# Band scores of a two-axis transformer block: every 128-key block in two 64-key halves

## The chip, the cores and the metric

One core of a Trainium2 chip runs the whole kernel. The metric is the device time of one launch in microseconds (us). Five engines run their own instruction streams side by side and meet at semaphores: TensorE (PE, matrix products; its weight loads are listed apart as PEld), VectorE (DVE), ScalarE (ACT), GpSimd (POOL) and the queue that issues transfers (SP).

## The reference, cut to what matters

The input `x` is 2 x 256 x 128 x 128 in fp32 (batch, time, band, channel). Three residual steps follow one another, each with its own layer norm: attention along time with a causal mask, attention along the 128 bands with a band mask, and a feed-forward with 512 hidden channels and gelu.

```python
bm = _band_mask(x.shape[2], BAND)      # 0 where |i - j| <= 16, else -inf
xt = _ln(x, ln_t_w, ln_t_b).transpose(0, 2, 1, 3)
x = x + _mha(xt, t_wi, t_bi, t_wo, t_bo, H_T, cm).transpose(0, 2, 1, 3)
xf = _ln(x, ln_f_w, ln_f_b)
x = x + _mha(xf, f_wi, f_bi, f_wo, f_bo, H_F, bm)
xn = _ln(x, ln_n_w, ln_n_b)
h = jax.nn.gelu(xn @ w1.T + b1, approximate=False)
x = x + (h @ w2.T + b2)
```

There are 4 heads of 32 channels. In the attention over bands, each of the 2 x 256 time steps is a sequence of 128 bands. A query attends only to keys within 16 bands of it, so a set of 64 keys meets at most 64 + 16 queries inside its block of 128.

## The kernel before, in words

Everything is fp32. The work is cut into groups of four sequences, 512 tokens each (`NT = 4` blocks of `P = 128`). First come 128 groups of attention over time (`OverTime`), then, for each run of 32 time steps, 8 groups of attention over bands (`OverBands`) followed by 8 groups of feed-forward (`FeedForward`); there are 16 such runs, so 128 groups of each kind. The band and feed-forward runs begin near 941 us of the profiled execution.

`BoundedPath.run` (L1057) writes the order out by hand as a software pipeline. Each step `n` of its loop does the scores of group `n`, the weighting of group `n-1`, the output product of group `n-2`, the projections of group `n+1`, and on VectorE the normalisation of a group three or more steps ahead. `InOrder` (L871) pins every instruction to that program order on its engine, so each engine works off its list as written.

For a band group the steps matter in this order:

- `queries_keys`, `take_query`, `take_key`, `values`, `take_values` (L576 to L602): TensorE projects the queries, keys and values; ScalarE copies them from PSUM to `qT`, `kT` and `v`. `qT` and `kT` hold head `h` in partitions 32h to 32h+31 and the 512 tokens along the free axis.
- `scores` (L764): TensorE multiplies keys by queries, one PSUM bank per head. A product for head `h` reads 32 rows. Its keys are the stationary operand and its queries the moving one, and the keys decide which PSUM partitions are written.
- `first_function` (L778): for the last head, VectorE clamps the scores and adds the mask in PSUM (a SCALAR_TENSOR_TENSOR, bank<-bank,band). ScalarE then exponentiates the four heads one after the other into `pf`.
- `first_mask` (L788): for the other three heads GpSimd sets the entries outside the band to zero by two affine selects each.
- `weigh` (L802) in the next step: TensorE sums the weights (`pf,ones`) and multiplies them into the values (`pf,v`).
- `invert` and `divide` (L607, L620): ScalarE takes ln and exp for the reciprocal (`r`), and VectorE does three passes that end in `oT`.
- `output` and `finish` (L635, L641) in the step after: TensorE multiplies `oT` by the output weights, and VectorE adds the result to the residual.

Between these, VectorE normalises a later group (four TENSOR_SCALAR into `xh`), transposes 32 x 32 squares into `z` (STREAM_TRANSPOSE), and in some steps takes the statistics of a group five steps ahead (`stats`, then `mv`). SP writes `z` to DRAM (`turned`) and reads it back as `xnT`.

A run's bands are numbered 0 to 7 here. In the loop the statistics of the feed-forward group `n+5` are taken in the steps of bands 3 to 7, because those feed-forward groups begin right after band 7. For the first run the band statistics, too, fall into its own steps (`due`, L1074).

PSUM has eight banks, handed out in turn by `bank` (L918). A band step takes ten turns: four for the scores, two held for a later output and query, and one each for `rp`, `op`, `kp` and `vp`. Thus a bank comes back one step later, and a product into it waits until its last reader is done. At the end of a run, where a feed-forward takes four turns and the projections are absent, `rp` of band 7 lands on the bank of `rp` of band 6.

In the scores before, the first and the last of the four blocks are done in two halves of 64 keys, each against 80 queries. The two middle blocks are done whole, 128 keys against 128 queries:

```python
for i, part in ((0, HALF), (1, P), (2, P), (3, HALF)):
    reach = 0 if part == P else BAND
```

Of the kernel before, what the change touches and what calls it, by code (L numbers as in the profile page):

```python
# [19 lines left out]
P = 128  # L20
H = 4
D = 32
BAND = 16
EPS = 1e-5
NEG = -1e38
NT = 4
# [6 lines left out]
HALF = P // 2  # L33
# [613 lines left out]
def rows_of(h):  # L647
    return slice(h * D, (h + 1) * D)
# [109 lines left out]
class OverBands(Attention):  # L758
# [5 lines left out]
    def scores(self, heads):  # L764
        path = self.path
        self.sp = {h: path.bank([P, NT * P], "sp") for h in heads}
        for i, part in ((0, HALF), (1, P), (2, P), (3, HALF)):
            reach = 0 if part == P else BAND
            for e in range(0, P, part):
                a = i * P + (e - reach if e else 0)  # L770
                q, keys = slice(a, a + part + reach), slice(i * P + e, i * P + e + part)
                for h in heads:
                    r = rows_of(h)
                    path.tensor.matmul(
                        self.sp[h][e : e + part, q], self.kT[r, keys], self.qT[r, q], start=True, stop=True
                    )

    def first_function(self):  # L778
# [459 lines left out]
```

## Time and profile before

| | us |
|---|---|
| median of 3 runs | 2713.04 (2712.95 to 2713.34) |
| profiled execution, its own time | 2711.64 |
| its span, first to last instruction | 2709.8 |
| PE busy | 2682.0 (99%) |
| DVE busy | 2195.4 (81%) |
| POOL busy | 1952.3 (72%) |
| ACT busy | 1854.5 (68%) |

The page comes from one execution of the program. A group of instructions is named by engine, operation, output and inputs, with partitions x elements; `32*64` on a matmul means 32 contracted rows and 64 stationary columns. Almost all instructions carry the line L881, the line of the helper that pins the order, so they are told apart by names and shapes. An fp32 product appears as two records of a weight load and two of a matmul. A matmul's end is modelled, so the starts of the records are the firm times. The granted TensorE clock was 0.998.

### The profile page before, as it was taken

To read this page: it belongs to the slowest core of one execution; us is meant where nothing else is said; L and a number is where in the kernel's file an instruction comes from. 1 tells how busy PE (TensorE), PEld (TensorE's weight loads), DVE (VectorE), ACT (ScalarE), POOL (GpSimd) and SP (SyncE) were. 2 spreads that over 40 slices of the span, in tenths; PEclk is the share of its full clock that TensorE was granted. 3 is DMA by queue.
4 is the path that set the end of the run, shared out by engine and by line. 5 is a ranking of instruction groups with operands and counts; after the bars stand their busy time and mean duration, and the time that the engine had idled before them with its cause. 6 is when DMAs were issued, how large, how long until landed. Compare 5 with 4: busy or idle time off the path is not lost.

```text
span 2709.8 us, 152534 instructions
## 1 busy us (share of the span) xinstructions
PE 2682.0 (99%) x66614; PEld 1805.8 (67%) x66614; DVE 2195.4 (81%) x6708; ACT 1854.5 (68%) x3620; POOL 1952.3 (72%) x2297
## 2 busy tenths in 40 slices
PE   7999999999999999999999999999999999999998
PEld 5666666666666666666666666666666666666666
DVE  6888989888988896977968769778687696886874
ACT  5999999999999865564655745646556466465563
POOL 4999999999999885766666657566676575665762
PEclk9999999999999999999999999999999999999999
DMA  5556555555555444444445444454454444544533
GB/s 147 149 150 157 148 151 153 155 148 149 152 154 150 124 112 122 124 111 122 115 119 128 112 120 120 112 131 108 119 131 108 124 121 111 131 108 117 132 94 82
DMA packets 471495, 346.83 MB, mean 128 GB/s; under 512 B 43296, under 2 KB 405152, under 8 KB 470816
## 3 DMA queue, kind: packets, MB, share of 16 engines
q1 hardware_dynamic: 469568, 335.92, 48.0%
q8 instruction: 524, 8.59, 1.4%
q14 instruction: 155, 1.27, 0.2%
q10 hardware_dynamic: 1248, 1.05, 0.2%
HBM read 169.03 MB, written 167.77 MB: 124 GB/s over the span
## 4 chain that ended last, share of the span: by engine, by line
PE 87%; DVE 10%; DMA 1%; ACT 1%; issue 0%; POOL 0%; SPq 0%; DVEq 0%; ACTq 0%
PE bank L881 87%; DVE xh L881 2%; DVE bank L881 2%; DVE stats L881 1%; DVE u L881 1%; DVE z L881 1%; DVE x L881 1%; DVE oT L881 1%; DMA xnT<-turned 1%; DVE mv L881 0%; DMA x<-in_x 0%; ACT p L881 0%; DVE vy L881 0%; DMA rows_sb<-in_rows 0%; DVE res L881 0%
## 5 line engine op out<-in xcount | busy, mean ns | idle before, releaser
L881 ACT ACTIVATE hT<-bank,b 128x512 f32<-128x512 f32 x512 | 347.1, 688 | 526.5 <-PE bank L881 507.7
L881 POOL TENSOR_SCALAR_AFFINE_SELECT pf<-pf 128x512 f32<-128x512 f32 x768 | 478.6, 638 | 289.5 <-ACT pf L881 263.0
L881 DVE TENSOR_SCALAR xh<-x,mv,rstd 128x160 f32<-128x160 f32 x1536 | 597.0, 431 | 14.3
L881 PEld LDWEIGHTS bank<-w2T_sb,hT 128*32 128x32 f32 x16384 | 457.1, 110 | 63.2 <-issue 39.7
L881 PE MATMUL bank<-xnT,wf 128*32 128x512 f32 x4096 | 488.7, 594 | 3.0 <-ACT p L881 3.0
L881 PE MATMUL bank<-w2T_sb,hT 128*32 128x128 f32 x16384 | 474.3, 273 | 0.2 <-ACT hT L881 0.2
L881 PE MATMUL bank<-xnT,w1f 128*32 128x512 f32 x4096 | 472.7, 592 | 0.0
L881 ACT ACTIVATE p<-bank 128x512 f32<-128x512 f32 (+1 forms) x1024 | 430.7, 494 | 38.4 <-PE bank L881 27.2
L881 POOL TENSOR_SCALAR_AFFINE_SELECT p<-p 128x1024 f32<-128x1024 f32 (+2 forms) x384 | 365.2, 951 | 86.0 <-ACT p L881 77.6
L881 DVE TENSOR_TENSOR res<-bank,res 128x512 f32<-128x512 f32 x256 | 175.9, 687 | 288.5 <-PE bank L881 229.8
L881 PE MATMUL bank<-qT,kT 32*64 32x80 f32 (+5 forms) x14336 | 363.5, 288 | 3.8 <-DVE oT L881 2.4
L881 PEld LDWEIGHTS bank<-qT,kT 32*64 32x64 f32 (+1 forms) x14336 | 288.8, 138 | 85.5 <-ACT kT L881 49.0
L881 PEld LDWEIGHTS bank<-wf,xnT 128*32 128x32 f32 x8192 | 233.6, 110 | 157.4 <-issue 102.8
L881 POOL TENSOR_TENSOR p<-p,p 128x512 f32<-128x512 f32 x256 | 324.5, 1289 | 10.7
L881 ACT ACTIVATE pf<-bank 128x512 f32<-128x512 f32 x512 | 264.5, 602 | 92.7 <-PE bank L881 92.1
L881 DVE BATCH_NORM_STATS2 stats<-x 128x6 f32<-128x128 f32 x1536 | 326.5, 275 | 0.4 <-DMA x<-in_x 0.4
L881 DVE STREAM_TRANSPOSE z<-xh 128x512 f32<-128x512 f32 x384 | 273.3, 712 | 13.5
L881 PEld LDWEIGHTS bank<-xnT,w1f 128*32 128x32 f32 x4096 | 150.5, 110 | 193.9 <-issue 168.7
L881 POOL TENSOR_TENSOR rstd<-rstd,mhalf 128x4 f32<-128x4 f32 x248 | 257.0, 1036 | 20.7
L881 PE MATMUL bank<-wf,xnT 128*32 128x128 f32 x8192 | 271.6, 273 | 0.0
L881 PE MATMUL bank<-wn,oT 128*32 128x128 f32 x8192 | 271.5, 273 | 0.0
L881 POOL TENSOR_SCALAR rstd<-mv 128x4 f32<-128x4 f32 x248 | 56.8, 229 | 297.1 <-DVE mv L881 296.6
(97 smaller groups left out, 3654.4 us busy)
## 6 DMA issues: line engine op xcount, KB each, us to landing
turned<-z SPq DMA_DIRECT2D x1536, 64.0 KB, 2.4
xnT<-turned SPq DMA_DIRECT2D x384, 256.0 KB, 3.0
x<-in_x SPq DMA_DIRECT2D x128, 256.0 KB, 4.2
x<-res SPq DMA_DIRECT2D x256, 128.0 KB, 2.5
x<-x SPq DMA_DIRECT2D x128, 256.0 KB, 4.3
out<-res SPq DMA_DIRECT2D x256, 128.0 KB, 2.5
w1T_sb<-in_w1T ACTq DMA_DIRECT2D x1, 256.0 KB, 6.0
w2T_sb<-in_w2T ACTq DMA_DIRECT2D x1, 256.0 KB, 7.1
```

Source lines behind the costliest of these rows:

```text
L881: return self.tc.keep_in_program_order(emit(*args, **kwargs))
```

## The change

Only `OverBands.scores` changes. All four blocks are now done in two 64-key halves against 80 queries: the first half meets queries 0 to 79 of its block, the second queries 48 to 127. Per group that makes 32 products of 32*64 in place of 16 of 32*64 and 8 of 32*128. The loop stays block by block, then half by half, then the four heads. The order of all other instructions is the same on every engine, and the products of the attention over time keep their own table.

```diff
-        for i, part in ((0, HALF), (1, P), (2, P), (3, HALF)):
-            reach = 0 if part == P else BAND
-            for e in range(0, P, part):
-                a = i * P + (e - reach if e else 0)
-                q, keys = slice(a, a + part + reach), slice(i * P + e, i * P + e + part)
+        for i in range(NT):
+            for e in range(2):
+                keys = slice(e * HALF, (e + 1) * HALF)
+                a = i * P + e * (HALF - BAND)
+                q = slice(a, a + HALF + BAND)
                 for h in heads:
                     r = rows_of(h)
                     path.tensor.matmul(
-                        self.sp[h][e : e + part, q], self.kT[r, keys], self.qT[r, q], start=True, stop=True
+                        self.sp[h][keys, q], self.kT[r, i * P + e * HALF : i * P + (e + 1) * HALF], self.qT[r, q],
+                        start=True, stop=True,
                     )
```

In the middle blocks, the corners of a bank that no product writes any more keep what the bank held before; the clamp with the mask and the two selects cover them, as they did in the first and last block.

## The prediction

> **What bounds the kernel now.** I read the page first, for which engine is full.
>
> ```profile
> PE 2682.0 (99%) x66614; PEld 1805.8 (67%) x66614; DVE 2195.4 (81%) x6708; ACT 1854.5 (68%) x3620; POOL 1952.3 (72%) x2297
> PE 87%; DVE 10%; DMA 1%; ACT 1%; issue 0%; POOL 0%; SPq 0%; DVEq 0%; ACTq 0%
> ```
>
> TensorE is full over the span and carries most of the chain that ended last, but VectorE carries a tenth of it. So the question is where. In a band step of a run's middle (the starts of the tensor records from 1527.098 to 1533.736 us) TensorE never pauses: scores 1305 ns, `pf,ones` 883, `pf,v` 873, output 873, queries and keys 1717, values 987; 6.638 us a step. The same step in the list of VectorE's instructions in order of time:
>
> ```profile
> 1528.73 0.70 DVE L881 SCALAR_TENSOR_TENSOR bank<-bank,band 128x512 f32<-128x512 f32 x1
> 1529.34 1.60 DVE L881 TENSOR_SCALAR xh<-x,mv,rstd 128x160 f32<-128x160 f32 x4
> 1530.97 0.71 DVE L881 STREAM_TRANSPOSE z<-xh 128x512 f32<-128x512 f32 x1
> 1531.61 0.83 DVE L881 BATCH_NORM_STATS2 stats<-x 128x6 f32<-128x128 f32 x4
> 1532.35 0.36 DVE L881 BATCH_NORM_AGGREGATE mv<-stats 128x2 f32<-128x6 f32 x4
> 1532.63 0.66 DVE L881 TENSOR_TENSOR x<-bank,x 128x512 f32<-128x512 f32 x1
> 1533.21 0.69 DVE L881 TENSOR_TENSOR bank<-bank,r 128x512 f32<-128x512 f32 x1
> 1533.93 0.69 DVE L881 SCALAR_TENSOR_TENSOR u<-bank,r 128x512 f32<-128x512 f32 x1
> 1534.66 0.69 DVE L881 TENSOR_TENSOR oT<-bank,u 128x512 f32<-128x512 f32 x1
> 1535.39 0.70 DVE L881 SCALAR_TENSOR_TENSOR bank<-bank,band 128x512 f32<-128x512 f32 x1
> ...
> 1554.60 0.69 DVE L881 TENSOR_TENSOR oT<-bank,u 128x512 f32<-128x512 f32 x1
> 1555.21 1.60 DVE L881 TENSOR_SCALAR xh<-x,mv,rstd 128x160 f32<-128x160 f32 x4
> ```
>
> No line names an idle time: VectorE is as full as TensorE. From `oT` to the next instruction it takes 0.73 us at 1534.66 but only 0.61 at 1554.60, where nothing is waited for. So about 0.1 us of the step is a wait for the scores, and VectorE's own step is 6.66 - 0.12 = 6.54. A second reading agrees: in the thirteenth run the mask starts 677, 579, 469 and 377 ns after the scores' end in four successive steps, so VectorE, once late, gains 0.10 a step. This holds for bands 3 to 7, which carry the statistics; earlier steps lack 1.02 us of them and do show idle time.
>
> Last, the chain between 1520 and 1570 us, at the end of the run:
>
> ```profile
> 1522.05 0.04 issue
> 1522.09 0.70 DVE bank L881
> ...
> 1553.87 0.70 DVE u L881
> 1554.58 0.14 issue
> 1554.71 15.34 PE bank L881 x389
> ```
>
> From the mask of band 3 to `u` of band 6 the chain stays on VectorE. Then `pf,ones` of band 7, which needs the bank that `u` read, waits for it: 740 ns from the last record before it, where this kind of product is otherwise followed at 382. All 16 runs have this gap (711 to 816).
>
> **What the Trainium skill says.** TensorEngine Tiling (Array Packing), Key Properties: a change of tiling mode drains TensorE, while tiles of one mode work independently. The trace agrees. The last record before the scores starts 203 ns before their first, against 92 at a boundary without a change; the middle blocks start 158 after the last record of the first block. TensorE: Matmul & The Clock Gate, LDWEIGHTS, has a load take its columns over 1.2 GHz: 53 ns for 64, 107 for 128. The second batch of records of the first block starts 120 ns after the first batch, which is 53 + 67 (two passes of 80 columns at the page's 2.4 GHz); in the middle blocks 213 = 107 + 107, and then 112, the load being hidden. The same page, under "Wait — 56ns, not 53.3ns?", has a floor of about 25 ns from matmul to matmul. Here the eight tiles' records start 6.7 ns apart in a batch, so a batch contradicts it; a rival below asks whether a long series does.
>
> **The change, part by part.**
>
> Removed: 16 records of 32*128 and two mode changes inside the scores. By starts, the 1305 ns are 324 (first block and the way out of it), 657 (middle blocks and out) and 324 (last block and out to `pf,ones`).
>
> Added: 32 records of 32*64 with 80 columns. All 64 records now run in one mode: eight batches of eight tiles. The first batch to the second is 120 as now. The last batch to `pf,ones` is 204 as now (1509.107 to 1509.311). Between lie six batch intervals that the trace does not have. I take 72: two passes of 80 are 66.7, plus the 5 that separate 112 from 106.7. The time scores support hidden loads, since their closing 64-column products follow one another on a tile at 58 ns where two passes are 53. The lower bound is 67. The upper is 120, nothing hidden. Sum: 120 + 6 x 72 + 204 = 756, so **0.549 us less per band group**; with 120, 0.261; with 67, 0.579.
>
> Moved: nothing. ScalarE, VectorE, GpSimd and SP keep their instructions and their order, and no transfer is added. No wait is added; the existing ones meet a TensorE that comes earlier. The exponentials start 0.2 us after the scores end; the copy of `v` before them ends 0.75 after the scores start, just before the new end at 0.756. So they follow. `kT`, for which the scores wait, depends on products whose length stays. GpSimd needs 5.2 us a step (3.94 of selects, 1.27 for `rstd`), below any step considered. The saved 0.549 would be complete at the end if VectorE kept up.
>
> It does not. TensorE's step becomes 6.09, VectorE's stays 6.54 in bands 3 to 7. Steps 0 to 2 need at most 5.52 of VectorE, so it follows TensorE up to the mask of band 3: four scores, 4 x 0.549 = 2.20. From there it runs alone and gains only what it waits now, four times 0.10 (masks of bands 4, 5, 6, 7). `u` of band 6 thus comes 2.60 earlier, and so does `pf,ones` of band 7. TensorE's remaining 4 x 0.549 - 0.4 = 1.8 turns into waits: first for a score bank read by `finish`, or for `oT`, which now precedes its product by 1.4; then at `pf,ones`. Nothing later in the run changes: `oT` of band 7 still precedes its product by 0.8, and feed-forward steps leave VectorE spare time.
>
> If VectorE's cover were gone, the price of those waits would be 0, and the run would gain 8 x 0.549 = 4.39.
>
> First run: its own statistics make VectorE late already. Its masks start up to 1.48 us after the scores and TensorE stalls in two score sections (2470 and 2052 ns). The mask of band 1 is the last that waits for TensorE, so I count 2 x 0.549 = 1.1. Sum: 15 x 2.60 + 1.1 = 40.1. Since VectorE's own delays now show (0.35 in the thirteenth run), I take off 0.5: **39.6 us**. Against the profiled execution's 2711.64 that is 2672.0. The median lies 1.4 above that execution: **2673.5**.
>
> **Rivals.**
>
> - *Loads are not hidden, or products come slower in a long series* (intervals up to 120): 4 x 0.261 + 0.4 = 1.44 a run; 15 x 1.44 + 0.5 = 22, time 2691. For it: no series of 80-column batches on 64-column tiles exceeds two now. Against: the 58 ns above.
> - *VectorE is not the limit*, and the run gains 4.39: 16 x 4.39 = 70, time 2643. The gap at `pf,ones` in all 16 runs and the 0.10 recovered speak against it.
> - *Nothing arrives*: 32 products take what 32 take in the time scores, whose 64 records span 1161 ns, 18.4 a record. With 63 x 18.4 + 158 = 1317 the scores would cost 12 ns more, 1.5 us in all, time 2714.5. Against: those tiles stream 640 columns in four passes, 1067 ns of the 1161, so streaming explains them.
> - *Slower*: at the score section, records in a long series keep the page's floor of 25 ns. Then 63 x 25 + 158 = 1733, 0.428 more, 128 times: 55 us, time 2768. It decides from 18.2 ns a record, where the section is 1305 again. The 18.4 of the time scores, themselves a long series, is below 25 and speaks against it; 9 would be needed.
>
> **How the numbers follow.** The likeliest case has 0.70. Its own range is 2670 to 2682: 0.58 a section gives 15 x 2.72 + 1.2 = 42, and 0.42, half of the batch interval's doubt, gives 15 x 2.08 + 0.8 - 0.5 = 31.5. Exposed loads have 0.12, no limit by VectorE 0.06, nothing 0.06, slower 0.06. A change under 0.2%, about 5.4 us, could not be told from none. So faster is 0.88, the same 0.06, slower 0.06. From 2664 to 2694 the range takes in the first two cases, with 6 us below the first for a VectorE step that is 0.1 shorter than read (60 steps), and leaves out the others.
>
> **What the profile after would show.** Score sections of 756 ns in one mode, with 64 records instead of 48: 8192 of 32x80 in place of 4096, and none of 32*128 in place of 2048. Band steps of about 6.09 for bands 1 to 3, then 6.54. New waits of TensorE for VectorE, together about 15 x 1.8 us beyond the present ones. VectorE's share rising, since its work is the same over a shorter span. Wrong would be a batch interval far from 72, a step below 6.5 in bands 4 to 7, or a stall of another engine: ScalarE's copy of `v` ending after the scores.

## The result and the profile after

The changed kernel takes 2684.02 us (median of 5 runs, 2680.03 to 2687.25) against 2712.95 us for the kernel before (5 runs). The ratio is 0.9896, with a 95% interval of 0.9882 to 0.9911: 28.9 us less, where 39.6 were forecast. The profiled execution took 2680.03 us with a span of 2678.2, so it lies 4 us below the median; the two profiled spans differ by 31.6 us.

The page of the changed kernel, the engines' busy times and the chain that ended last by engine:

```profile
PE 2639.5 (99%) x68662; PEld 1801.7 (67%) x68662; DVE 2190.0 (82%) x6708; ACT 1856.2 (69%) x3620; POOL 1951.5 (73%) x2297
PE 80%; DVE 15%; DMA 2%; issue 1%; SPq 1%; ACT 0%; DVEq 0%; ACTq 0%
```

TensorE has 2048 matmul records more and is busy for 42.5 us less. VectorE's work is the same, and its share of the chain has grown from 10 to 15%. VectorE's instructions in order of time, bands 3 to 7 of one run, of which the mask alone is shown (start, length, and idle time before it in brackets):

```profile
1509.35 0.70 DVE L882 SCALAR_TENSOR_TENSOR bank<-bank,band 128x512 f32<-128x512 f32 x1 [0.36 <-PE bank L882]
...
1515.89 0.69 DVE L882 SCALAR_TENSOR_TENSOR bank<-bank,band 128x512 f32<-128x512 f32 x1
...
1522.41 0.69 DVE L882 SCALAR_TENSOR_TENSOR bank<-bank,band 128x512 f32<-128x512 f32 x1
...
1528.94 0.69 DVE L882 SCALAR_TENSOR_TENSOR bank<-bank,band 128x512 f32<-128x512 f32 x1
...
1535.47 0.69 DVE L882 SCALAR_TENSOR_TENSOR bank<-bank,band 128x512 f32<-128x512 f32 x1
```

Only the mask of band 3 waits for TensorE. The others follow at 6.52 to 6.54 us, which is VectorE's own step. The chain at the end of that run, and TensorE's instructions there:

```profile
1509.31 0.04 issue
1509.35 0.70 DVE bank L882
...
1540.66 0.70 DVE u L882
1541.36 0.14 issue
1541.50 18.78 PE bank L882 x433
```

```profile
1537.29 3.60 PE L882 MATMUL bank<-xnT,w1f 128*32 128x512 f32 x30
1541.50 1.07 PE L882 MATMUL bank<-pf,ones 128*32 128x512 f32 x8 [0.61 <-DVE u L882]
1542.35 1.08 PE L882 MATMUL bank<-pf,v 128*32 128x128 f32 x32
```

The chain has its old form: from the mask of band 3 to `u` of band 6 on VectorE, then over to `pf,ones` of band 7. That product now starts 1367 ns (mean of 16) after the record before it, where it was 744. The list of TensorE's waits in the stretch of bands and feed-forward (us in total, times, longest) has it 16 times:

```profile
PE bank L882 <- DVE u L882: 12.4, 16, 0.8
```

What did not come as forecast is the score section. One of them before, and one after, each with the product behind it:

```profile
1508.01 1.38 PE L881 MATMUL bank<-qT,kT 32*64 32x80 f32 x48
...
1509.31 1.06 PE L881 MATMUL bank<-pf,ones 128*32 128x512 f32 x8
```

```profile
1514.38 1.09 PE L882 MATMUL bank<-qT,kT 32*64 32x80 f32 x64
...
1515.40 1.06 PE L882 MATMUL bank<-pf,ones 128*32 128x512 f32 x8
```

The first line counts all 48 records of the section, the 16 with 128 keys too. From first start to first start, outside the first run, the section lasts 983 ns on average for the bands 0 to 6, and 1094 for band 7, instead of 1306 before and 756 in the forecast. The medians over the sections show where it leaves the forecast (ns after the section's first record; a batch is eight records):

| record | 1 | 9 | 17 | 25 | 33 | 41 | 49 | 57 | 64 |
|---|---|---|---|---|---|---|---|---|---|
| forecast | 0 | 120 | 192 | 264 | 336 | 408 | 480 | 552 | 599 |
| changed kernel | 0 | 120 | 189 | 258 | 328 | 517 | 619 | 712 | 837 |

Through the 33rd record the forecast holds within 8 ns. From there the records come singly and unevenly: the first gap is 55 ns, and the last 31 records take 509 ns, 16 to 17 a record on average, with 409 to 582 in single sections. Their modelled length is often 276 ns instead of 228, like that of the first batch, which waits for its loads.

From one run's `pf,ones` of band 7 to the next run's, TensorE needs 109.13 us before and 107.35 after: 1.78 less, 26.7 in 15 runs. The first run, from its first score record to its `pf,ones` of band 7, is 1.0 us shorter (56.50 before, 55.50 after). The two profiled executions already differ by 4.1 us at that first score record, ahead of any changed instruction. There the execution of the kernel before had two stretches at a lower granted TensorE clock, 0.72 between 38 and 44 us and 0.74 between 942 and 948 us, and that of the changed kernel had 1.00 where it ran the same instructions (36 to 44 and 939.5 to 945.5 us). The same product just ahead of the first score section, before and after:

```profile
945.74 1.94 PE L881 MATMUL bank<-p,ones 128*32 128x256 f32 x16
```

```profile
942.82 1.07 PE L882 MATMUL bank<-p,ones 128*32 128x256 f32 x16
```

So of the 31.6 us between the two profiled spans about 27.5 belong to the change.

### The profile page after: what moved, and what is told of

Read it like the earlier page. It is cut to its first block, busy times and chain, and to the rows that moved or that the text cites. A ratio compares the mean times of both kernels' runs of the same rounds, so it can differ in the third digit from the quotient of the medians.

```text
span 2678.2 us, 156630 instructions
## 1 busy us (share of the span) xinstructions
PE 2639.5 (99%) x68662; PEld 1801.7 (67%) x68662; DVE 2190.0 (82%) x6708; ACT 1856.2 (69%) x3620; POOL 1951.5 (73%) x2297
## 4 chain that ended last, share of the span: by engine, by line
PE 80%; DVE 15%; DMA 2%; issue 1%; SPq 1%; ACT 0%; DVEq 0%; ACTq 0%
PE bank L882 80%; DVE xh L882 3%; DVE bank L882 3%; DVE stats L882 2%; DVE z L882 2%; DVE u L882 2%; DMA xnT<-turned 1%; DVE x L882 1%; DMA turned<-z 1%; DVE mv L882 1%; SPq L882 1%; DVE oT L882 0%; ACT p L882 0%; DVE vy L882 0%; DVE res L882 0%
## 5 line engine op out<-in xcount | busy, mean ns | idle before, releaser
L882 ACT ACTIVATE p<-bank 128x512 f32<-128x512 f32 (+1 forms) x1024 | 430.6, 494 | 37.9 <-PE bank L882 26.7
L882 PE MATMUL bank<-qT,kT 32*64 32x80 f32 (+4 forms) x16384 | 323.7, 273 | 4.0 <-DVE oT L882 2.4
L882 PEld LDWEIGHTS bank<-qT,kT 32*64 32x64 f32 x16384 | 275.9, 131 | 58.2 <-ACT kT L882 48.4
L882 PEld LDWEIGHTS bank<-xnT,w1f 128*32 128x32 f32 x4096 | 156.8, 110 | 189.3 <-issue 158.3
```

Source lines behind the costliest of these rows:

```text
L882: return self.tc.keep_in_program_order(emit(*args, **kwargs))
```

## The experiments

The supply theory for the second half of a section: TensorE has 32 records ready when the scores may start (each a load and a matmul, so 64 instructions), and afterwards they reach it one by one, 17 ns apart. The Trainium skill gives TensorE a queue of 64 instructions (TensorE: Matmul & The Clock Gate, the table at the head of the page), which is this number; that this queue is what holds them is an assumption of the theory. For the end of a run the theory is the forecast's: VectorE decides when `pf,ones` of band 7 starts.

### Blocks in reverse

```diff
-        for i in range(NT):
+        for i in reversed(range(NT)):
```

> The changed kernel with the four blocks of a score section in the order 3, 2, 1, 0; nothing else. Theory (supply): from the 33rd record on, products start no faster than about 17 ns a record because TensorE has used up what stood ready in its queue. Then nothing changes: four batches 120, 69, 69 ns apart whatever the blocks, the last record at a median near 840 ns after the first, time within 3 us of 2684. Rival (place): blocks 2 and 3 are slow wherever they stand, because of their columns in the banks or in qT and kT. Then the first 32 records spread (the 32nd near 510 ns instead of 305) and the last 32 run in tight batches.

Measured: 2684.49 us (one run). The records 1, 9, 17, 25, 33, 41, 49, 57, 64 start at 0, 120, 189, 258, 328, 518, 619, 711, 838 ns, the row of the changed kernel again. The limit goes with the record's number and not with the block.

### A pause in the middle of the section

```diff
+    def take_key(self):
+        path = self.path
+        self.kT = path.work.tile([P, NT * P], F32, name="kT")
+        path.scalar.copy(self.kT[:, 0 : 2 * P], self.kp[:, 0 : 2 * P])
+
+    def take_values(self):
+        super().take_values()
+        self.path.scalar.copy(self.kT[:, 2 * P :], self.kp[:, 2 * P :])
```

> The changed kernel with kT copied in two halves: columns 0 to 255 where the copy stands now, columns 256 to 511 after the copy of v. Blocks 2 and 3 so wait in the middle of the section, until about 1.1 us after its start. Theory (supply): TensorE's queue fills again in that pause, and the last 32 records run like the first 32, from their first to their last about 305 ns (254 if the loads have been done in the pause). Rival (place, or a limit that a section reaches after its first 32 records whatever happens between): they stay at 16 to 17 ns a record, about 500 ns from first to last. Time under both: 0.5 to 0.6 us more per band group, 2740 to 2765 us.

Measured: 2740.77 us (one run). TensorE's instructions in one step of this kernel, the wait in brackets, show the two halves of the section as two groups of equal length:

```profile
1524.07 0.53 PE L891 MATMUL bank<-qT,kT 32*64 32x80 f32 x32
1525.12 0.54 PE L891 MATMUL bank<-qT,kT 32*64 32x80 f32 x32 [0.52 <-ACT kT L891]
```

In the medians the last 32 records start at 1050, 1170, 1240 and 1309 ns by batch, 310 ns from first to last, where the first 32 take 305 and where the changed kernel takes 509. After a pause in which TensorE waits, at least 32 records are ready again; more were not left in the section. A limit of place, or one that only the length of the series brings, is excluded. The changed kernel's own trace shows the same count: in its first run the section of band 1 waits before its 7th record and those of bands 3 to 7 wait before their 5th, and the first gap of 55 ns comes behind the 38th and behind the 36th record, each time the 32nd from the wait.

### Wider products

```diff
-                a = i * P + e * (HALF - BAND)
-                q = slice(a, a + HALF + BAND)
+                q = slice(i * P, (i + 1) * P)
```

> The changed kernel with every half against all 128 queries of its block, so 32 products of 128 columns; same result. A tile then needs 107 ns a record and eight tiles 14 ns a record, less than the 17 of the supply. Theory (supply by count, 32 records stand ready and the rest come at 16 to 17 ns each): batches 112 apart up to the 32nd record, the 33rd near 496, the last near 1010, a section near 1170. Theory with a queue that fills again during the longer batches: all batches 112 apart, a section near 1070. Rival (something that breaks about 330 ns into the section, whatever the records): irregular starts from the 20th record on. Time 2685 to 2700 us.

Measured: 2694.64 us (one run). The batches start at 0, 160, 269 and 378 ns, the 33rd record at 488, the 64th at 990 (median) or 1010 (mean); the section is 1208 on average, over the expected 1170 because the way from the last record to `pf,ones` takes 197 instead of 158. That is the supply by count: the break comes within three records behind the 33rd although that one is reached 160 ns later, and the last 31 take 502 ns, about as with 80 columns (509). Streams of 107 ns on eight tiles would have needed 14 ns a record, so the tiles aren't what limits. But a queue that took in a record every 17 ns while the first 32 ran would have been given some 29 more by 488 ns, and the break would have come later. So the count is shown; what delivers the records, and that it is the queue of 64, is not.

### Halves side by side, with the old products

```diff
-        for i, part in ((0, HALF), (1, P), (2, P), (3, HALF)):
+        for i, part in ((0, HALF), (3, HALF), (1, P), (2, P)):
```

> The kernel before with its four blocks in the order 0, 3, 1, 2: the same 24 products, but the two blocks in halves stand side by side, so one change of mode less. From the pieces: four batches of halves at 120 and 69 ns and the way out, 258 + 204 = 462, then the whole blocks 657 as before; 1119 ns a section instead of 1305. Supply does not limit it: 32 records stand ready, and the whole blocks take 28 ns a record. Time: 0.186 less a section; over a run TensorE gains 1.49 and VectorE, which keeps its 6.53 in bands 3 to 7, allows 4 x 0.186 + 0.1 + 4 x 0.1 = 1.24; 20 us, ratio near 0.9925. Rival (shorter sections come from the narrower products alone, and a change of mode costs nothing): 1305 and no gain.

Measured: 2689.39 us (2 runs), ratio 0.9922 (0.9903 to 0.9941). TensorE's instructions of one step:

```profile
1524.43 1.19 PE L881 MATMUL bank<-qT,kT 32*64 32x80 f32 x48
1525.55 1.06 PE L881 MATMUL bank<-pf,ones 128*32 128x512 f32 x8
```

From first start to first start the section is 1120 ns, as added up from the pieces. So with the products of the kernel before, one change of mode less and loads hidden over four batches are worth 186 ns together; the run doesn't part the two. The changed kernel takes a further 137 off in bands 0 to 6. So the reordering alone has most of the gain in time: 20.6 us of medians, against 28.9.

### Statistics behind the divide

In the step of band 7 alone, the statistics of a later feed-forward group are moved on VectorE. The same move is made in the kernel before.

```diff
-            do_at(n + 5, FeedForward, "statistics")
+            last = bands[2] and feeds[3]
+            if not last:
+                do_at(n + 5, FeedForward, "statistics")
...
             do(n - 1, "divide")
+            if last:
+                do_at(n + 5, FeedForward, "statistics")
```

> The changed kernel with one VectorE item moved: in the step of band 7 alone, the statistics of the feed-forward group five steps ahead come after divide instead of before it; same work, same result. Theory (VectorE decides when pf,ones of band 7 may start, through u of band 6): u comes 1.02 us earlier in each run, the wait there (about 0.98 us beyond a normal gap) goes, and the next VectorE product that TensorE needs, oT of band 7, which now precedes its product by 0.75, becomes the limit. Gain about 0.75 us a run, 12 us in all: 2672 us, ratio to before near 0.985. Rival (the wait there is due to GpSimd's selects or ScalarE's exponentials of band 7): no gain, 2684.

> The kernel before with the same item moved, to tell what of that gain is the move's own. Theory: the wait of 0.36 us a run goes, 16 times: 5.8 us, 2707 us, ratio near 0.998. So of the 12 us in the changed kernel about half is there only because the score sections became shorter. Rival: 0.

Measured: 2670.34 us, ratio 0.9858 (0.9843 to 0.9874), for the changed kernel with the move; 2705.52 us, ratio 0.9979 (0.9972 to 0.9986), for the kernel before with it. In the first, TensorE's and VectorE's instructions at the end of a run:

```profile
1534.48 3.62 PE L882 MATMUL bank<-xnT,w1f 128*32 128x512 f32 x32
1537.91 1.04 PE L882 MATMUL bank<-pf,ones 128*32 128x512 f32 x8
...
1545.73 1.94 PE L882 MATMUL bank<-xnT,w1f 128*32 128x512 f32 x16
1547.65 0.54 PE L882 MATMUL bank<-wn,oT 128*32 128x128 f32 x12
```

```profile
1537.00 0.69 DVE L882 SCALAR_TENSOR_TENSOR u<-bank,r 128x512 f32<-128x512 f32 x1
...
1547.17 0.43 DVE L882 TENSOR_SCALAR oT<-u 128x512 f32<-128x512 f32 x1
```

`u` of band 6 ends at 1537.69, before TensorE gets to `pf,ones`, and the gap at `pf,ones` has fallen to 409 ns. The next one in line is `oT` of band 7: it ends at 1547.60, and its product starts 0.05 us later, 581 ns after the last record instead of 382. So a run is 0.71 us shorter than in the changed kernel (106.63 against 107.35), where the forecast of this experiment had 0.75. In the kernel before the same move makes a run 0.35 us shorter (108.78 against 109.13), so half of its worth comes with the shorter score sections. The wait came from VectorE; the selects of GpSimd and the exponentials of ScalarE were left as they were.

### Without the clamp

> The changed kernel without VectorE's clamp and band mask of the last head (one SCALAR_TENSOR_TENSOR of 0.70 us a band step is left out, so that head is unmasked). Theory: VectorE's step in bands 3 to 7 falls from 6.53 to about 5.93, below TensorE's 6.31, and all waits of TensorE for VectorE in the run go: 0.98 at pf,ones and about 0.1 in the scores of band 7, 16 times, 17 us: 2667. Rival (VectorE costs TensorE nothing beyond what it cost before): 2678 or more.

> The kernel before with the same item left out. Theory: only the wait of 0.36 a run goes, 5.8 us: 2707. The difference to the changed kernel without it, 40 us, is then the shorter score sections alone, 128 x 0.3 = 38 us; with VectorE's clamp in place 29 of it arrive.

```diff
-        for h in range(H - self.by_vector, H):
-            sp = self.sp[h].rearrange("p (i q) -> p i q", i=NT)
-            path.vector.scalar_tensor_tensor(
-                sp, sp, LIMIT, path.band.unsqueeze(1).to_broadcast([P, NT, P]), ALU.min, ALU.add
-            )
```

Measured: 2664.91 us, ratio 0.9834 (0.9819 to 0.9850), for the changed kernel without it; 2703.93 us, ratio 0.9977 (0.9969 to 0.9986), for the kernel before without it. The page of the former has the chain almost wholly on TensorE:

```profile
PE 97%; DVE 1%; DMA 0%; ACT 0%; issue 0%; POOL 0%; SPq 0%; DVEq 0%; ACTq 0%
```

Outside the first run all score sections are then alike, 959 to 983 ns by band, band 7's too, whose 1094 thus held about 0.1 us of waits for VectorE. The three pairs of kernels give what the shorter sections are worth:

| VectorE's work | before, us | changed, us | difference |
|---|---|---|---|
| as it is | 2712.95 | 2684.02 | 28.9 |
| statistics of one step later | 2705.52 | 2670.34 | 35.2 |
| without the clamp | 2703.93 | 2664.91 | 39.0 |

With VectorE out of the way all of 128 x (1309 - 976) ns = 43 us could show, and 39 do. As it is, VectorE keeps about 10 of these 39; the waits at `pf,ones` agree, which grew by 0.62 us a run, 10 us in all 16.

### One more step later

The statistics are also moved behind the divide in the first feed-forward step of a run.

```diff
-            last = bands[2] and feeds[3]
+            last = turn or bands[2] and feeds[3]
```

> The changed kernel with the statistics after divide in two steps of a run: band 7's, as in the earlier run, and the first feed-forward step's. Theory: in the earlier run TensorE waits 0.2 us a run (581 ns before the output product of band 7 instead of 382 to 409) for oT of band 7, the next VectorE product in line; with 1.02 us of statistics moved behind it that wait goes: 0.18 x 16 = 3 us, 2667 us, ratio near 0.9848. Rival: something else is late in its place, for example the rstd of the next group: no gain or a loss.

Measured: 2668.37 us, ratio 0.9847 (0.9833 to 0.9861). The gap before the output product of band 7 is 409 ns instead of 581, so the wait is gone. In time the kernel can't be told from the one with a single move (0.9858), since the intervals overlap. It is the fastest kernel here that computes everything.

## Why the prediction was right or wrong

**What bounds the kernel.** Right. VectorE's step in bands 3 to 7 was read as 6.54 us and measured 6.52 to 6.54 once it ran alone. The end of a run's chain passes through `u` of band 6, and both experiments that relieve VectorE take the wait away.

**The sum over a run.** Its form was right, its main term mis-sized. With the 0.32 us that the first four sections in fact save (1306 - 983), and the 4 x 0.10 of VectorE, it gives 1.68; measured are 1.78. The mask of band 3 now starts on average 0.27 us after the scores instead of 0.35, which is most of the missing tenth. TensorE's surplus over VectorE is then not 1.8 us a run but about 0.7: 0.62 appear at `pf,ones`, and 0.1 in the scores of band 7. The 2684 us lie outside the 2670 to 2682 that the likeliest case gave itself, since a section saves less than the 0.42 at its lower end; they lie inside the whole range only because that range was drawn to take in the rival with exposed loads as well.

**The step that failed** is the added part, "six batch intervals" of 72 ns. The first three after 120 are 69, 69 and 70; then the records come at 16 to 17 ns each, and the section is 983 rather than 756, so 0.32 is saved and not 0.549. The evidence I took for hidden loads, the closing products of the time scores at 58 ns, is of products that follow one another on one tile; it says nothing of a long series on eight. The rival with intervals up to 120 (0.261 a section, 2691 us) had the right size, but its first half has the wrong cause: the lengths of 276 ns fit exposed loads, yet only past the 33rd record, where the loads may come late too; from the second batch up to there the intervals of 69 ns leave no room for them. Its other half, products that come slower in a long series, is what happens.

**The rival "nothing arrives"** took 18.4 ns a record from the time scores, and I set it aside because streaming explained that number. It was closer to the truth than that: past the 33rd record the mean pace is 16 to 17. It cost little, since half of a section runs at 69 ns a batch. Whether the time scores, too, are held in this way was not tried.

**The slower rival** was wrong: the longest series of the changed section runs at 16 to 17 ns a record and not at 25. **The rival without a limit by VectorE** was wrong too: a run gained 1.78 us and not 4.39, and TensorE's wait for `u` grew by 0.62.

**The first run** was put at 1.1 us and brought 1.0. The size is right, but not its making: the sections of bands 0 and 2, which don't wait, went from 1305 to 896 ns there, so a section saves 0.41 and not 0.549, and twice that is 0.8. Why the records past the 33rd come faster in the first run (411 ns for the last 31) isn't settled.

**Other engines.** No new wait of TensorE for ScalarE or GpSimd above 0.2 us appeared; the copy of `v`, feared to come too late, has more room in a section of 983 ns than in one of 756.

## What to carry to other kernels

Where two engines are equally full, a cut on one is worth only what the other allows, and the place where they meet next (here a bank that VectorE still reads) can be found in the profile before. Then an item moved behind that meeting point, without any work saved, gives most of what a cut gives: one move on VectorE in 1 of 16 steps of a run brought the changed kernel from 0.9896 to 0.9858, and leaving the clamp out brought it to 0.9834. When products are made smaller, count the records as well as the columns: here a burst of 8.6 ns a record on eight tiles did not carry on past the 33rd record of a series.

## What the runs showed of the hardware that was not expected

- After a wait, TensorE runs 32 records (32 loads and 32 matmuls) in batches 69 ns apart, 8.6 ns a record with 80 columns on eight tiles. The following ones come 16 to 17 ns apart on average, with 80 columns as with 128 (13 to 19 in single sections with 80). After a pause of 0.75 us the next 32, all that were left, ran fast again. That nothing seems to be added while the first 32 run, even when they take 488 ns, was not explained.
- Putting two equal tile shapes side by side instead of at both ends of a series, with the same 24 products, took 186 off 1305 ns.
